# Graph layer with two adjacency relations: from neighbour sums first to weight products first, with a list scheduler

## The chip, the core and the metric

The kernel runs on one core of one Trainium2 chip. The metric is the device time of a whole execution in microseconds, the median of several runs. A shape such as 128x256 in a profile row is partitions x elements per partition.

## The reference, cut to what matters

There are B = 64 graphs of L = 256 tokens with H = 768 features, and a 0/1 adjacency matrix per graph (about 1.6% ones).

```python
h = jnp.maximum(_layernorm(x, axis=-1), 0.0)
...
ctx = jnp.matmul(adj, hs @ Wadj.T + badj) / deg_c[..., None]
ctx = ctx + jnp.matmul(radj, hs @ Wrev.T + brev) / rdeg_c[..., None]
ctx = ctx + hs @ Wself.T + bself
agg = jnp.einsum('bij,bijr->bir', adj, E[rels])
rel = agg @ Wr.T + br * deg[..., None]
...
x = x + (ctx + rel)
```

Here hs is h, radj is adj turned over, deg and rdeg are their row sums, and rels is adj itself. Since adj holds 0 and 1, the relation terms shrink to a few rank-one rows: token degree times a row of length 768. A second program path for other adjacency values (`general_path`) is compiled in and skipped by a branch on a flag.

## The kernel before, in words

Per graph, three 256 x 768 left matrices (the two neighbour sums `A h / deg` and `A' h / rdeg`, and h itself) meet three 768 x 768 weights. `PRODUCTS` is a fast 3x3 block scheme: the 2x3 blocks a0..b2 of left rows (tokens 0-127 are a, 128-255 are b; 0, 1, 2 is which left matrix) times the 3x3 blocks of weights (which relation, which third of the output columns) in 15 products in place of 18. Each product is [128 x 768] by [768 x 256], six matmul steps of contraction 128, and each is added to or taken from several output blocks.

The work is an order written out by hand, in two sweeps over the 64 graphs, because not all combined weights `W[n]` fit beside the rest.

- Sweep 1 (`step1`, `ORDER1`, eight products): while the products of graph M run on PE, `others_of_step` makes the left matrices of graph M+1 (`self_features` L391 on POOL, `aggregate` L400: 24 matmuls 128x512 in fp32r on a high and a low part of h, evicted by DVE at L405), and the statistics, transpose (`spread`, L340) and normalisation (L362) of graph M+2. `combine_left` (L417) builds sums of left blocks on POOL. `store_left` writes the left matrices to DRAM on ACT's queue; partial outputs go out on SP's queue.
- Sweep 2 (`step2`, `ORDER2`, seven products): left matrices and partial outputs come back. From graph 2 on, four of the seven products (9, 7, 15, 4) are done in 12-bit words: `split_left` (L431 to L434) cuts the left operand into three fp32r words, `split_right` has cut the weights, and `product_first` (L457), a rescale of the PSUM bank on ACT (L460) and `product` (L469) add three fp32r products. The other products are fp32 matmuls (L469), which PE executes as two instructions each. `add_out` (L482, L484) adds banks to the output on DVE.
- Rank-one rows are one fp32r matmul each (L474). DMA issues come from SP and ACT.

`spread` also sends per-token factors through DRAM: `d` out (L347), then `row` back, broadcast to all partitions (L349).

Of the kernel before, what the change touches and what calls it, by code (L numbers as in the profile page):

```python
# [9 lines left out]
F32 = mybir.dt.float32  # L10
F32R = mybir.dt.float32r
BF16 = mybir.dt.bfloat16
# [5 lines left out]
P = 128  # L18
EPS = 1e-5
NMEAN, RSTD, RDEG, RRDEG = 8, 9, 10, 11  # L20


STEP = 4096.0
LOWER = 1.0 - 2.0**-13

# [7 lines left out]
    11: ("a1", "-12 +22 +10"),  # L35
# [7 lines left out]
    13: ("a0", "-00 +20 +02"),  # L43
    1: ("b0", "-00 +10 +01"),
# [3 lines left out]
LEFT1 = {  # L48
    "b0+b1": ("b0", ALU.add, "b1", "t0"),
    "b2-a1": ("b2", ALU.subtract, "a1", "t1"),  # L50
    "a1+b1": ("a1", ALU.add, "b1", "t2"),
    "a1+b0+b1": ("a1+b1", ALU.add, "b0", "b0"),
    "a0+a1+b0+b1": ("a0", ALU.add, "a1+b0+b1", "b1"),
    "a2+b2": ("a2", ALU.add, "b2", "a2"),
}
LEFT2 = {
    "a0+a2": ("a0", ALU.add, "a2", "a0"),
    "a1+a2": ("a1", ALU.add, "a2", "a1"),
    "a0+a2+b2": ("a0+a2", ALU.add, "b2", "a2"),
    "b1+b2": ("b1", ALU.add, "b2", "b1"),  # L60
    "a0+a2+b0+b2": ("b0", ALU.add, "a0+a2+b2", "a0+a2"),
}

ROWS = ((0, 1, None), (1, 2, None), (0, None, 2), (0, 2, 0), (1, None, 1), (1, 1, 0))

ORDER1 = (
    (5, "y", None, ((1, 1, 0),)),
    (10, "z", None, ((1, 1, 2),)),  # L70
    (8, "y", None, ((1, 1, 2),)),
    (11, "w", None, ((-1, 0, 2),)),
    (14, "y", 2, ((-1, 0, 2),)),
    (3, "w", 1, ((1, 1, 2),)),
    (13, "y", 3, ((-1, 0, 0),)),
    (2, "z", 0, ((1, 0, 1),)),
)
ORDER2 = (
    (7, "v", None, None),
    (9, "x", None, ((1, 0, 0),)),  # L80
    (15, "u", None, None),
    (7, "v", None, ((1, 0, 1, 2),)),
    (6, "x", None, ((1, 0, 1),)),
    (15, "u", None, ((1, 1, 1, 2),)),
    (4, "t", None, None),
    (12, "x", 4, ((-1, 1, 1),)),
    (4, "t", None, ((-1, 0, 1), (1, 1, 1))),
    (9, "x", None, None),
    (1, "x", 5, ((-1, 1, 0),)),
)  # L90


WORDS = {9: (5, 10), 7: (8, 11), 15: (14, 3), 4: (13, 2)}
LEFT_WORDS = (("x", "t0"), ("a", "a", "t1"), ("adj", "row", "t2"))
# [3 lines left out]
def kernel(  # L98
# [14 lines left out]

# [7 lines left out]
    NB = H // 3  # L146
# [3 lines left out]
    xt_v = x_t.rearrange("b (f p) i -> b p f i", p=P)  # L150
# [10 lines left out]
    others = const.tile([P, B], F32, name="others")  # L161
    flag = const.tile([1, 1], I32, name="flag")

    def main_path(main: ExitStack):
        pool1 = main.enter_context(tc.tile_pool(name="pool1", bufs=1))
        pool2 = main.enter_context(tc.tile_pool(name="pool2", bufs=2))
        pool3 = main.enter_context(tc.tile_pool(name="pool3", bufs=3))
        dram = main.enter_context(tc.tile_pool(name="dram", bufs=3, space=bass.MemoryType.DRAM))
        kept = main.enter_context(tc.tile_pool(name="kept", bufs=1, space=bass.MemoryType.DRAM))
        ps3 = main.enter_context(tc.tile_pool(name="ps3", bufs=3, space=bass.MemoryType.PSUM))  # L170
        ps1 = main.enter_context(tc.tile_pool(name="ps1", bufs=1, space=bass.MemoryType.PSUM))
        sweep = ExitStack()
        ps_sums = sweep.enter_context(tc.tile_pool(name="ps_sums", bufs=2, space=bass.MemoryType.PSUM))

        W = {n: pool1.tile([P, F, NB], F32, name=f"w{n}") for n in PRODUCTS}
        rows = pool1.tile([P, len(ROWS), NB], F32R, name="rows")

        hilo = pool1.tile([P, 2, C, H], F32R, tag="hilo", name="hilo")
        xT = pool1.tile([P, F, L], F32, tag="xT", name="xT")
        tok = [pool1.tile([P, C, NROW], F32, name=f"tok{i}") for i in range(2)]  # L180
        cols = [pool1.tile([P, C, 64], F32, name=f"cols{i}") for i in range(2)]

        def load_weights(products):
            for n in products:
                right = PRODUCTS[n][1]
                k, o = int(right[1]), int(right[2])
                v = (wadj_t, wrev_t, wself_t)[k].rearrange("(f p) o -> p f o", p=P)
                nc.sync.dma_start(W[n], v[:, :, ts(o, NB)])

        single = {right[1:]: n for n, (_, right) in PRODUCTS.items() if len(right) == 3}  # L190
        turned = set()

        def turn(n):

            if PRODUCTS[n][1][0] == "-" and n not in turned:
                nc.scalar.activation(W[n], W[n], AF.Copy, scale=-1.0)
                turned.add(n)

        def combine_weights(n, eng):

            first, *others = PRODUCTS[n][1].split()
            if not others:
                turn(n)
            for k, other in enumerate(others):
                m = single[other[1:]]
                turn(m)
                if other[0] == PRODUCTS[m][1][0]:
                    if first[0] == "-" and k == 0:
                        eng.tensor_tensor(W[n], W[m], W[n], op=ALU.subtract)
                    else:  # L210
                        eng.tensor_tensor(W[n], W[n], W[m], op=ALU.add)
                else:
                    assert first[0] == "+" or k > 0
                    eng.tensor_tensor(W[n], W[n], W[m], op=ALU.subtract)  # L214

        R = {}

        def load_rows():
            sizes = {"full": len(ROWS) * NB, "brow": H, "pick": 2 * P, "eT": NREL}
            work = pool2.tile([P, sum(sizes.values())], F32, tag="X", name="rows_work")  # L220
            wr = pool2.tile([P, 2, H], F32, tag="Xs", name="rows_wr")
            at = 0
            for n, size in sizes.items():
                R[n] = work[:, at : at + size]
                at += size
            for k in range(2):
                R[f"wr{k}"] = wr[:, k, :]
            nc.gpsimd.memset(work[:, : at - NREL], 0.0)
            R["full"] = R["full"].rearrange("p (k n) -> p k n", n=NB)
            R["pick"] = R["pick"].rearrange("p (k n) -> p k n", n=P)  # L230
            brow = R["brow"]
            nc.sync.dma_start(R["eT"], e_t)
            nc.sync.dma_start(R["wr0"], wr_t)
            nc.sync.dma_start(R["wr1"], wrr_t)
            for q in range(4):
                nc.sync.dma_start(brow[q * 32 : q * 32 + NROW, :], bias)

        def prepare_rows():


            eT, brow, pick = (R[n] for n in ("eT", "brow", "pick"))
            wr = R["wr0"], R["wr1"]
            for k, at in ((0, 1), (1, NBASE + 1)):
                to = pick[:, k, :].rearrange("p (q r) -> p q r", q=4)[:, :, 3 + k]
                nc.scalar.activation(to, eT[:, at : at + 1].to_broadcast([P, 4]), AF.Copy)
            for n in range(2):
                pr = ps_sums.tile([P, 512], F32, tag="pa", name=f"pr{n}")
                for k in range(2):
                    nc.tensor.matmul(pr[:, :HO], pick[:, k, :], wr[k][:, ts(n, HO)], start=(k == 0), stop=(k == 1))
                nc.vector.tensor_add(brow[:, ts(n, HO)], brow[:, ts(n, HO)], pr[:, :HO])  # L250

        def place_rows():
            brow, full = R["brow"], R["full"]
            hi = W[1].bitcast(F32R)
            for c in range(C):
                at = slice(c * 64, (c + 1) * 64)
                for k, (of, plus, minus) in enumerate(ROWS):
                    if of == c and minus is None:
                        nc.scalar.activation(full[at, k, :], brow[at, ts(plus, NB)], AF.Copy)
                    elif of == c and plus is None:  # L260
                        nc.scalar.activation(full[at, k, :], brow[at, ts(minus, NB)], AF.Copy, scale=-1.0)
                    elif of == c:
                        nc.gpsimd.tensor_tensor(
                            full[at, k, :], brow[at, ts(plus, NB)], brow[at, ts(minus, NB)], op=ALU.subtract
                        )
            nc.scalar.activation(hi, full, AF.Copy)
            nc.gpsimd.tensor_tensor(rows, full, hi.bitcast(F32), op=ALU.subtract)
            for q in (0, 2):
                at = slice(q * 32, (q + 1) * 32)
                nc.scalar.activation(rows[at], hi[at].bitcast(F32), AF.Copy)  # L270

        S = [{} for _ in range(B)]

        def load_x(b):
            s = S[b]
            s["x"] = pool1.tile([P, C, H], F32, tag="x", name=f"x_{b}")
            nc.sync.dma_start(s["x"], x_v[b])
# [560 lines left out]
```

## Time and profile before

| | us |
|---|---|
| runs (three) | 2934.51, 2949.36, 2957.05 |
| median | 2949.36 |
| profiled execution, span | 2930.6 |
| sweep 1, most graphs, transpose to transpose (L340) | 26.9 |
| sweep 1, the slower graphs | up to 28.5 |
| sweep 2, from the fourth graph on, start of product 7 to the next | 16.6 |
| the first three intervals of sweep 2 | 24.8, 29.3, 25.0 |

The profiled execution is its own run; its span is 2930.6 us, 18.8 us below the median. Rows of groups read: line, engine, operation, output <- inputs, shape, count, then busy us and mean ns of one, then idle time of the engine before them and what ended it. Rows of the timeline read: start us, length us, engine, line, operation. Matmuls are pipelined: the time that one takes from the stream is the distance between starts and not the length shown.

### The profile page before, as it was taken

What the parts mean: (1) busy time and instruction counts of PE and PEld (TensorE: products, weight loads), DVE (VectorE), ACT (ScalarE), POOL (GpSimd) and SP (SyncE); (2) the same over time, 40 slices, a digit from 0 to 9 for tenths busy, and PEclk for the clock granted to TensorE, in tenths of its full rate; (3) what the DMA queues carried; (4) which work ended last, traced back from release to release, by engine and by line L of the source; (5) the groups of instructions that cost most, each with busy time, mean ns of one, the idle gap of its engine ahead of it and who ended that gap; (6) DMA issues with size and microseconds to landing.
All of it is one profiled execution on the core that took longest, in us unless ns stands there. A gap on an engine that the chain in (4) does not pass through costs nothing.

```text
span 2930.6 us, 39745 instructions
## 1 busy us (share of the span) xinstructions
PE 2821.0 (96%) x15002; PEld 2504.8 (85%) x15002; DVE 1748.8 (60%) x2968; ACT 1027.8 (35%) x2045; POOL 1809.4 (62%) x905
## 2 busy tenths in 40 slices
PE   4699999999999999999999999799999999999999
PEld 3588888888888888888888888689999999999998
DVE  6655555555555655556556663666666666666665
ACT  3222223223223223322223221244445444444443
POOL 4566677676666676766666666355555555555553
PEclk8899999999999999999999999999999999999999
DMA  8667777677677677776666665466766666676664
GB/s 286 226 221 243 249 250 252 238 246 251 234 249 244 229 245 254 248 238 239 227 244 232 233 237 200 172 232 239 250 236 247 243 238 249 234 252 236 245 242 155
DMA packets 226444, 695.08 MB, mean 237 GB/s; under 512 B 17332, under 2 KB 94900, under 8 KB 209864
## 3 DMA queue, kind: packets, MB, share of 16 engines
q1 hardware_dynamic: 189384, 390.49, 40.2%
q10 hardware_dynamic: 36864, 302.01, 27.0%
q8 instruction: 120, 1.97, 0.3%
q14 instruction: 76, 0.62, 0.1%
HBM read 436.31 MB, written 256.11 MB: 236 GB/s over the span
## 4 chain that ended last, share of the span: by engine, by line
PE 78%; POOL 6%; DMA 6%; DVE 5%; ACT 3%; issue 1%; ACTq 0%; SPq 0%; POOLq 0%; DVEq 0%
PE x L469 18%; PE y L469 18%; PE w L469 9%; PE pa L400 8%; PE z L469 7%; POOL xT L391 6%; DMA row<-d 4%; PE x L457 3%; PE u L457 3%; PE v L457 3%; PE t L457 3%; PE t L469 2%; PE u L469 1%; PE v L469 1%; ACT a L309 1%; DVE cols L330 1%
## 5 line engine op out<-in xcount | busy, mean ns | idle before, releaser
L417 POOL TENSOR_TENSOR X<-X,Xs 128x768 f32<-128x768 f32 x256 | 469.6, 1853 | 500.0 <-DVE words L433 435.6
L391 POOL TENSOR_TENSOR xT<-xT,row 128x1536 f32<-128x1536 f32 (+1 forms) x128 | 445.9, 3484 | 192.0 <-DMA row<-d 187.0
L469 PE MATMUL y<-w,X 128*128 128x256 f32 x2304 | 534.7, 382 | 4.6 <-POOL X L417 4.1
L469 PEld LDWEIGHTS y<-w,X 128*128 128x128 f32 x2304 | 431.3, 191 | 71.2 <-POOL X L417 4.9
L400 PE MATMUL pa<-a,hilo 128*128 128x512 f32 x1536 | 453.3, 431 | 27.2 <-DVE X L405 24.1
L392 ACT ACTIVATE Xs<-xT 128x1536 f32<-128x1536 f32 x64 | 95.0, 1485 | 856.3 <-POOL xT L391 817.4
L469 PE MATMUL x<-w,X 128*128 128x256 f32 x1560 | 362.1, 382 | 14.7 <-POOL X L417 10.0
L400 PEld LDWEIGHTS pa<-a,hilo 128*128 128x128 f32 x1536 | 291.9, 191 | 91.1 <-DVE X L405 26.3
L469 PEld LDWEIGHTS x<-w,X 128*128 128x128 f32 x1560 | 289.6, 192 | 50.6 <-POOL X L417 10.4
L405 DVE TENSOR_TENSOR X<-pa,row 128x512 f32<-128x512 f32 x384 | 264.3, 689 | 112.8 <-PE pa L400 111.5
L432 ACT ACTIVATE top<-words 128x768 f32<-128x768 f32 x248 | 202.3, 816 | 248.9 <-DVE words L434 245.4
L362 DVE SCALAR_TENSOR_TENSOR hilo<-x,cols,hilo 128x768 fp32r<-128x768 f32 x128 | 261.8, 2046 | 9.6 <-ACT hilo L365 9.5
L434 DVE SCALAR_TENSOR_TENSOR words<-words,top 128x768 fp32r<-128x768 f32 x248 | 236.5, 954 | 8.6
L433 DVE TENSOR_TENSOR words<-X,top 128x768 fp32r<-128x768 f32 x186 | 177.1, 952 | 43.3 <-POOL X L417 34.9
L322 POOL TENSOR_TENSOR cols<-cols,half 128x2 f32<-128x2 f32 x64 | 44.8, 700 | 246.4 <-DVE cols L321 226.9
L469 PE MATMUL y<-w,b0+b 128*128 128x256 f32 x768 | 176.4, 379 | 2.6 <-POOL b0+b L417 2.6
L469 PE MATMUL z<-w,Xs 128*128 128x256 f32 x768 | 178.0, 382 | 0.0
L469 PE MATMUL z<-w,b2-a 128*128 128x256 f32 x768 | 176.2, 379 | 1.4 <-DVE w L214 1.4
L469 PE MATMUL w<-w,X 128*128 128x256 f32 x768 | 176.3, 379 | 0.0
L469 PE MATMUL w<-w,a1+b 128*128 128x256 f32 x768 | 176.2, 379 | 0.0
L469 PE MATMUL x<-w,Xs 128*128 128x256 f32 x768 | 176.1, 379 | 0.0
L469 PEld LDWEIGHTS z<-w,b2-a 128*128 128x128 f32 x768 | 145.4, 189 | 24.2 <-DVE w L214 1.8
(118 smaller groups left out, 4828.8 us busy)
## 6 DMA issues: line engine op xcount, KB each, us to landing
kept_X<-X ACTq DMA_DIRECT2D x64, 1536.0 KB, 5.1
X<-kept_X ACTq DMA_DIRECT2D x64, 1536.0 KB, 7.2
x<-in_x_dram SPq DMA_DIRECT2D x64, 768.0 KB, 5.2
xT<-in_x_t_dram SPq DMA_DIRECT2D x64, 768.0 KB
o<-in_x_dram SPq DMA_DIRECT2D x64, 768.0 KB
kept_Xs<-Xs ACTq DMA_DIRECT2D x64, 768.0 KB, 6.6
sums<-o SPq DMA_DIRECT2D x128, 384.0 KB, 7.0
Xs<-kept_Xs ACTq DMA_DIRECT2D x64, 768.0 KB, 9.4
```

Source lines behind the costliest of these rows:

```text
L322: nc.gpsimd.tensor_tensor(v[:, :, RSTD], v[:, :, RSTD], half, op=ALU.pow)
L362: nc.vector.scalar_tensor_tensor(lo, hx, rstd, hi.bitcast(F32), op0=ALU.mult, op1=ALU.subtract)
L391: eng.tensor_tensor(v, v, row[:, k : k + 1, :].to_broadcast([P, f1 - f0, L]), op=op)
L392: nc.scalar.activation(s["Xs"], xT, AF.Relu)
L400: nc.tensor.matmul(pa, hilo[:, part, c, ts(f, P)], s["a"][:, c, :, :].rearrange("p s i -> p (s i)"), start=(k == 0), stop=(k == 2 * C - 1),)
L405: nc.vector.tensor_mul(s["X"][:, f, :, :].rearrange("p s i -> p (s i)"), pa, s["row"][:, 2:4, :].rearrange("p s i -> p (s i)"))
L417: (eng or nc.gpsimd).tensor_tensor(L[name], L[x], L[y], op=op)
L432: nc.scalar.activation(top, words[0].bitcast(F32), AF.Copy)
L433: nc.vector.tensor_tensor(words[1], value, top, op=ALU.subtract)
L434: nc.vector.scalar_tensor_tensor(words[2], words[1].bitcast(F32), -STEP, top, op0=ALU.mult, op1=ALU.add)
L457: nc.tensor.matmul(ps, l[k][:, f, :], r[2 * k][:, f, :], start=(k == 0 and f == 0), stop=(k == 1 and f == F - 1))
L469: nc.tensor.matmul(ps, l[:, f, :], r[:, f, :], start=(start and f == 0), stop=(row is None and f == F - 1), skip_group_check=not start,)
```

## The change

The kernel is rewritten, with the same 15-product scheme and two sweeps of eight and seven products.

1. Weights come ahead of neighbour sums. The left operand of all 15 products is h itself (`a0..b2` are now thirds of h's features), the three relations stand side by side in the output columns, and each product is [128 x 256] by [256 x 768]. The neighbour sums are taken of the 768-wide results: `aggregate` multiplies adjacency blocks by a high and a low part (`high_low`) of the two neighbour relations' results, in sweep 2, and DVE scales by the inverse degree while adding.
2. All 15 products are in words. Each is three word pairs x two contraction steps x two halves of 384 columns = 12 fp32r matmuls, with a rescale of the bank on ACT between the pairs of different scale.
3. Between sweeps, h and five partial blocks per graph go to DRAM and return.
4. Every operation is recorded with a cost, a rank (due time plus a table `OFFSETS` of shifts by name) and its buffers. `Plan.schedule` orders the operations by list scheduling and assigns buffers; DVE operations with two SBUF inputs and POOL operations are recorded with a lock so that the plan never runs two of them at once. The program is emitted in that order; at run time each engine follows its own order and waits on semaphores.
5. All DMAs are issued by SP. `x_t` is laid out in tiles, and `dynamic_dma_scratch_size=1024` gives most of the DMA scratch to buffers.

The core of the diff:

```diff
-        def aggregate(b, f):
...
-                    nc.tensor.matmul(
-                        pa, hilo[:, part, c, ts(f, P)], s["a"][:, c, :, :].rearrange("p s i -> p (s i)"),
...
+SLOTS = {"W": 24, "B": 17, "T": 6, "A": 3, "S": 6, "Q": 4}
+PERIOD = (17.2, 21.4)
+PREPARE = (6.0, 4.5)
...
+    def split(b, n, s, rank):
+        src = combine(b, s, PRODUCTS[n][0], rank - LEAD - 1.0)
...
+            lambda: nc.scalar.activation(t(w)[:, 0], src[1](), AF.Copy, scale=LOWER),
...
+            lambda: nc.vector.tensor_tensor(t(w)[:, 1], src[1](), t(w)[:, 0].bitcast(F32), op=ALU.subtract), True,
...
+            lambda: nc.vector.scalar_tensor_tensor(
+                t(w)[:, 2], t(w)[:, 1].bitcast(F32), -STEP, t(w)[:, 0].bitcast(F32), op0=ALU.mult, op1=ALU.add
+            ), True,
...
+    def passes(b, n, w, q, pairs, start, stop):
+        r = words[n]
+        for i, (lw, rw) in enumerate(pairs):
+            for f in range(2):
+                for half in range(2):
+                    nc.tensor.matmul(
+                        t(q)[:, half, : H // 2], t(w)[:, lw, f, :], t(r[rw])[:, f, ts(half, H // 2)],
...
+        pe(took(first) + more(first), rank, f"first {n} {b}", reads_of(first), [q], lambda: run(first, place == 0, True, add(first)))
+        act(
+            on_act(H), rank + 1.0, f"scale {n} {b}", [q], [q],
+            lambda: nc.scalar.activation(view(), view(), AF.Copy, scale=scale),
+        )
+        pe(took(second) + more(second), rank + 2.0, f"second {n} {b}", reads_of(second), [q], lambda: run(second, False, True, add(second)))
...
+    def aggregate(b, s, k, pairs, rank):
+        for ic in range(C):
...
+                for c in range(C):
+                    for part in range(2):
+                        for half in range(2):
+                            nc.tensor.matmul(
+                                t(q)[:, half, : H // 2], t(s["a"])[:, c, k, ts(ic, P)], t(pairs[c])[:, part, ts(half, H // 2)],
...
-    nc = _bacc.Bacc("TRN2", target_bir_lowering=False, num_devices=1)
+    nc = _bacc.Bacc("TRN2", target_bir_lowering=False, num_devices=1, dynamic_dma_scratch_size=1024)
```

Per product, the reads of the bank (`read`) add it into blocks of 128x768: four of them in sweep 1 are first writes on ACT, the other four of sweep 1 and ten of sweep 2 are on DVE. `front1` centres h on POOL and normalises it on DVE (128x768 each, two per graph), with the token factors through `d` and `row` as before. `prepare` cuts each combined weight into three words at the start of each sweep (52 DVE operations of 128x768 in sweep 1, 38 in sweep 2).

## The prediction

> **What bounds the kernel now.** I read the page's busy shares first, then the table of stretches for one steady piece of each sweep, then the timeline of PE for what one matmul takes from the stream, then the groups by shape and the timelines of DVE, POOL and SP for prices.
>
> ```profile
> PE 2821.0 (96%) x15002; PEld 2504.8 (85%) x15002; DVE 1748.8 (60%) x2968; ACT 1027.8 (35%) x2045; POOL 1809.4 (62%) x905
> ```
>
> ```profile
> 150.00:688.00 538.00, 538.00 (x2501) 465.40 (x2500) 293.08 (x600) 157.40 (x369) 380.45 (x180) 1.00 0.70 243
> 2100.00:2432.00 332.00, 332.00 (x2210) 313.31 (x2209) 220.45 (x321) 159.56 (x262) 180.65 (x100) 1.00 0.68 242
> ```
>
> The columns are length, busy us of PE, PEld, DVE, ACT, POOL, granted clock, DMA share, GB/s. PE is busy for every microsecond of both stretches (20 graphs each: 26.9 us and 16.6 us per graph) at full clock; no other engine is over 71%. PE is the bound, if its matmuls are also packed:
>
> ```profile
> 109.67 2.22 PE L400 MATMUL pa<-a,hilo 128*128 128x512 f32 x8
> 111.73 2.75 PE L469 MATMUL y<-w,X 128*128 128x256 f32 x12
> 114.13 0.47 PE L474 MATMUL y<-rows,tokT 128*128 128x256 f32 x1
> 114.44 1.09 PE L400 MATMUL pa<-a,hilo 128*128 128x512 f32 x4
> 115.37 1.46 PE L469 MATMUL w<-w,a1+b 128*128 128x256 f32 x6
> ```
>
> ```profile
> 2001.09 1.59 PE L457 MATMUL u<-w,words 128*128 128x256 f32 x12
> 2002.52 0.87 PE L469 MATMUL v<-w,words 128*128 128x256 f32 x6
> ```
>
> Starts give the price. Fp32r, 512 wide: (115.37 - 114.44)/4 = 0.233. Fp32r, 256 wide: (2002.52 - 2001.09)/12 = 0.119. One fp32 product (12 instructions) with its row matmul: 114.44 - 111.73 = 2.71, so 2.59 for the product. Check: sweep 1 is 8 x 2.59 + 3 x 0.12 + 24 x 0.233 = 26.7 (26.9 seen), sweep 2 is 72 x 0.119 + 3 x 2.59 + 2 x 0.12 = 16.6 (16.6 seen). So 64 x 43.5 = 2784 of 2930.6 us is packed PE work. The other 147 us are the start (some 65), slower graphs in sweep 1 (up to 28.5 instead of 26.9; together 31), the first three intervals of sweep 2 (79.1 - 49.8 = 29), and rests at the end.
>
> **The change, part by part.**
>
> *PE work.* All fp32 products go. Per graph sweep 1 has 8 x 12 = 96 fp32r matmuls of 384 columns, sweep 2 has 7 x 12 + 32 (neighbour sums) + 6 (rows) = 122. No row has an fp32r matmul of 384; between 0.119 at 256 and 0.233 at 512 the straight line gives 0.176, and I take 0.177. Sweep 1: 96 x 0.177 + 0.2 for a transpose = 17.2. Sweep 2: 122 x 0.177 + 0.2 = 21.8. Together 39.0 against 43.5: -4.5 us per graph, 64 x 4.5 = -288 us. Here the Trainium skill (TensorE: Matmul & The Clock Gate, Back-to-back issue gap) says that a warm matmul takes N/2.4 + 2.5 ns: 162 ns at 384, 35.5 us per graph, and 220 us less in all than my 64 x 39.0 = 2496. Its rule fits the fp32 rows here (two passes of 256 in 0.216), but both fp32r rows stand 9% above it; the change is all fp32r, so I use the rows.
>
> *DVE, ACT, POOL.* The prices:
>
> ```profile
> L417 POOL TENSOR_TENSOR b0+b<-X 128x768 f32<-128x768 f32 x64 | 115.9, 1811 | 77.3 <-DVE X L405 77.3
> L432 ACT ACTIVATE top<-words 128x768 f32<-128x768 f32 x248 | 202.3, 816 | 248.9 <-DVE words L434 245.4 <-DVE o L484 1.4
> L433 DVE TENSOR_TENSOR words<-X,top 128x768 fp32r<-128x768 f32 x186 | 177.1, 952 | 43.3 <-POOL X L417 34.9 <-ACT top L432 8.3
> L482 DVE TENSOR_TENSOR o<-o,x 128x256 f32<-128x256 f32 x128 | 53.9, 421 | 162.3 <-PE x L469 162.2
> ```
>
> Busy us, then mean ns. DVE, sweep 1: 16 word cuts of 256 x 0.42 = 6.7; 4 reads of 768 x 0.95 = 3.8; 2 normalisations x 0.95 = 1.9; statistics 4 x 0.54 (L319) + 0.6 = 2.7: 15.1 of PE's 17.2. Sweep 2: 14 x 0.42 + 10 reads x 0.95 + 4 sums x 0.95 + 4 small x 0.2 = 20.0 of 21.8. In the trace independent DVE operations start 0.08 before the one ahead ends (L482 at 1002.44 + 0.42, the next at 1002.77), which takes off up to 2.4 and 2.6. DVE rises from 60% to 78-90%: under PE, with little to spare. ACT, sweep 1: 8 rescales and 4 first writes x 0.82, 8 first words x 0.37 (L460), 0.3: 13.1. Sweep 2: 11 x 0.82 + 7 x 0.37 + 6 conversions x 0.59 (L309 with its accumulator read) + 0.6 = 15.7. Under PE. POOL: 1.81 at 768 and 3.50 at 1536 (L391) give 0.70 at 256. Sweep 1: 6 x 0.70 + 2 x 1.81 + 0.70 (L322) = 8.5; sweep 2: 5 x 0.70 + 4 x 1.81 = 10.7.
>
> *DVE against POOL.* Today words are cut with one operand in PSUM (L433: 952 with POOL running or not). The new cuts and normalisations have two SBUF inputs, like L362, alone 1.01 (three cases at the start), mean 2.05:
>
> ```profile
> 1002.77 2.22 DVE L362 SCALAR_TENSOR_TENSOR hilo<-x,cols,hilo 128x768 fp32r<-128x768 f32 x1
> ```
>
> ```profile
> 1002.36 1.82 POOL L417 TENSOR_TENSOR a1+b<-X 128x768 f32<-128x768 f32 x1 [0.57 <-PE w L469]
> 1004.26 2.41 POOL L417 TENSOR_TENSOR X<-a1+b,X 128x768 f32<-128x768 f32 x1
> ```
>
> DVE is issued at 1002.77 and ends at 1004.99, 0.81 after POOL's end at 1004.18; POOL's next takes 2.41 instead of 1.82, 0.59 longer, though DVE still had 0.73 to run. The Trainium skill (SBUF — State Buffer, Who interferes with whom) says that the pair is held for the whole instruction. By that rule sweep 1 needs 16 x 0.42 + 1.9 + 8.5 = 17.1 us of the pair per graph, as much as PE's 17.2, and the plan would have to be perfect. By the row DVE gives it back about 0.15 early: 16 x 0.27 + 2 x 0.80 + 8.5 = 14.4. Sweep 2: 16.6 by the rule, 14.5 by the row, of 21.8. I take the row, with some stalls left (below).
>
> *Turn-around of a bank.* In sweep 2 today ACT starts 0.32 after the start of a product's last word matmul, which is 0.20 after its 0.119 slot, and PE can go on 0.05 after ACT. With a rescale of 0.82 that is 1.07 us between the two parts of a product. In the emitted order, the work that PE does before it returns to the same bank is 8 matmuls (1.42 us) at three returns of sweep 1 and 12 (2.12) or more at the others; sweep 2 is alike. So it fits when ACT is free, with 0.35 to spare at the shortest.
>
> *DMA.* Per graph sweep 1 moves 11 pieces of 0.39 MB and 0.26 for the row: 4.6 MB; sweep 2 4.5 MB. The stretches show 243 GB/s at a share of 0.70, 347 GB/s if full: 13.2 us of 17.2, and 12.9 of 21.8. All issues now stand in one queue, 13 per graph and sweep at about 0.37 us, 4.8 us. Each `row` holds it until `d` has landed:
>
> ```profile
> 862.16 0.93 SPq L347 DMA_DIRECT2D d<-line  x2
> 866.33 0.35 SPq L349 DMA_DIRECT2D row<-d  x1
> ```
>
> 3.9 us after the second `d` at 862.48. Behind it wait loads of x and h and stores of partial blocks, and for these DVE's statistics and POOL. The order puts two transfers (2.3 us of work) between `d` and `row`, so about 1.6 us of the engines' time is lost: 14.8 of 17.2. Hidden; if the cover goes it costs what exceeds 17.2. Smaller scratch: every issue in the new order is on SP, none on POOL, so I count it as nothing.
>
> *Start, middle, end.* `prepare` in sweep 1 is 52 DVE operations of 768. Back to back a 1536-wide one takes 1.67 (30.78 to 32.45, L214), so 0.87 each: 45 us, plus 6 for the first graph's own cuts and 11 for the statistics of five graphs that stand between them. DVE starts near 10, waits for DMA at first, and ends near 75 us. Only one graph and part of the second are done then: 55 lost, about as now (65). Sweep 2: 38 x 0.87 = 33, of which some goes under the last graphs of sweep 1: 28 lost, as now (29). End: last sums, adding, store and its landing (5.1 in the DMA issues): 10. Together 93.
>
> **The sum.** 64 x 39.0 = 2496, + 93 = 2589. Stalls: between none and 5 us per graph (rival B in full). Today's far less tight sweep 1 loses 31/64 = 0.5; I take 0.7, 45 us in all: 2634 as a profiled span. The profile's span is 18.8 us (0.6%) under the median of the runs, so the median would be 2650.
>
> **Rivals.**
>
> A, the forecast: PE stays the bound at 39.0-40.5 us per graph. For it: packed PE today, all other sums under PE's. 2590 to 2720.
>
> B, DVE and POOL hold each other up. For it: the row of L362, which doubles in nearly every case, and 32 such operations per graph. Against: the plan knows the lock, and the waits in today's trace repeat in the same places for every graph. If in each graph the 6 long POOL operations cost DVE half their time, 0.9, and the 11 short ones 0.35, DVE gets 9.3 us: 35.1 + 9.3 = 44.4 without overlaps, 39.4 with them. The middle, 41.9, is 2.9 over PE: 2589 + 64 x 2.9 = 2775, range 2720 to 2860.
>
> C, the one SP queue is late in sweep 1. For it: 14.8 of 17.2 and all stores in order. Against: nothing in sweep 1 loads what was just stored, except `row`. At 3.5 us over PE's 17.2: 2589 + 64 x 3.5 = 2813; 2720 to 2850.
>
> D, slower: the bank turn-around. If ACT has two other 0.82 operations ahead of a rescale, the 1.07 grow to 2.71, and three returns at 1.42 and five at 2.12 stall PE by 3 x 1.3 + 5 x 0.6 = 6.9 us in sweep 1, about 5.5 in sweep 2: 12.4 per graph, 2589 + 794 = 3383. It turns the sign from (2949 - 2589)/64 = 5.6 us per graph on, 0.37 us at each of 15 products. Against: ACT is at 72-76%, and its queue rarely holds two long ones in a row.
>
> E, the new words win nothing because fp32r matmuls with their loads don't hold 0.177 at 384 (0.20 would be enough): 64 x 218 x 0.023 = 321, 2910 + stalls, no change.
>
> **Chances.** A 0.62, B 0.21, C 0.08, E 0.03, D 0.06. The time is A's, 2650. A's own range 2590 to 2720; the range for 8 in 10 leaves out D, E and the upper part of B, and takes in a lower stall and a shorter start: 2570 to 2810. About 1% is what a measurement of this kernel can tell from no change. Faster by over 1% are A, B, C: 0.91; within 1% E: 0.03; slower D: 0.06.
>
> **What would show it.** PE starts 0.177 apart within a group of four; steady graphs 17.2-18 us apart in sweep 1 and 21.8-22.5 in sweep 2; PE busy all through them; DVE 78-90%. B would show as word cuts (256 wide) well over 0.42 and PE's longest waits on DVE; C as waits for `x`, `xt` or `row` landings; D as waits of PE on ACT's rescale. The forecast falls if a steady graph takes over 41 us, or if the start or middle lose over 40 us more than said.

## The result, and the profile after

| | us |
|---|---|
| before, median on the same chip | 2949.42 |
| after, median of four runs (2752.92 to 2768.15) | 2760.02 |
| ratio, with 95% interval | 0.9372 (0.9335 to 0.9409) |
| profiled execution of after, span | 2756.2 |
| sweep 1, mean distance from graph to graph (transposes L492, sixth to last but one) | 18.80 |
| sweep 2, the same (transposes L625) | 22.37 |

The change saves 6.3%. The forecast was 2650 with 2570 to 2810 around it; the time lies in the range, but 110 us above the point, and above the 2720 at which the likeliest case ended. It is rival B's size.

The top of the page of after, with the shares of the engines:

```profile
span 2756.2 us, 43346 instructions
PE 2545.2 (92%) x14090; PEld 2439.7 (89%) x14090; DVE 2444.6 (89%) x4013; ACT 1698.2 (62%) x3459; POOL 1322.4 (48%) x1160
```

Two stretches of after, one inside each sweep (length, busy us of PE, PEld, DVE, ACT, POOL, granted clock, DMA share, GB/s):

```profile
150.00:1100.00 950.00, 884.06 (x4910) 849.43 (x4909) 877.54 (x1466) 604.23 (x1063) 468.26 (x453) 0.99 0.72 245
1300.00:2600.00 1300.00, 1267.44 (x7077) 1219.60 (x7078) 1126.78 (x1851) 794.30 (x1827) 646.43 (x519) 1.00 0.58 197
```

Before, PE was busy in every microsecond of such stretches. Now it rests for 7% of the first and 2.5% of the second. DVE is busy for 92% of the first, a share that includes the time in which an issued operation only waits. The timeline of PE in sweep 1 of after gives the price of one matmul:

```profile
706.36 1.55 PE L406 MATMUL w<-word,left 128*128 128x384 f32 x8
707.75 1.55 PE L406 MATMUL y<-word,left 128*128 128x384 f32 x8
709.13 0.86 PE L406 MATMUL z<-word,left 128*128 128x384 f32 x4
```

The starts are 1.39 and 1.38 apart for eight matmuls: 0.173 each, where 0.177 was forecast. So PE is not slower than said; it waits. The waits of PE, over the whole execution of after (us in total, times, longest):

```profile
PE y L406 <- DVE c L462: 55.4, 35, 2.7
PE pt L492 <- POOL cols L489: 39.0, 3, 30.7
PE pt L625 <- DVE c L460: 26.1, 43, 1.7
PE y L406 <- DVE left L395: 16.4, 2, 15.9
PE w L406 <- DVE x L462: 12.8, 23, 1.6
```

Apart from the two lines with the waits of 30.7 and 15.9 us (the start), PE waits for DVE to read a product out of its PSUM bank (L460, L462), since the next product goes into that bank. Those reads are not slow themselves, as the groups of after by shape show (busy us, mean ns of one, idle before):

```profile
L395 DVE SCALAR_TENSOR_TENSOR left<-left 128x256 fp32r<-128x256 f32 x960 | 524.0, 552 | 25.9
L391 DVE TENSOR_TENSOR left<-b2-a,left 128x256 fp32r<-128x256 f32 x64 | 57.0, 891 | 2.5 <-ACT left L387 2.3
L391 DVE TENSOR_TENSOR left<-a0+a,left 128x256 fp32r<-128x256 f32 x64 | 26.7, 417 | 0.0
L462 DVE SCALAR_TENSOR_TENSOR c<-x,c 128x768 f32<-128x768 f32 x128 | 121.7, 951 | 5.6 <-PE x L406 2.9 <-ACT junk L614 0.5
```

A read takes its 0.95. The word cuts ahead of it in DVE's queue (two per left operand, L391 and L395) don't all take their 0.42: some groups do (417), others take twice that (891). The difference is whether POOL was at work on two SBUF inputs. One place shows it, in the timelines of DVE and then of POOL:

```profile
710.87 1.09 DVE L391 TENSOR_TENSOR left<-b2-a,left 128x256 fp32r<-128x256 f32 x1
712.00 0.85 DVE L395 SCALAR_TENSOR_TENSOR left<-left 128x256 fp32r<-128x256 f32 x1
712.76 2.59 DVE L515 SCALAR_TENSOR_TENSOR h<-h,row 128x768 f32<-128x768 f32 x1
715.28 0.41 DVE L391 TENSOR_TENSOR left<-h,left 128x256 fp32r<-128x256 f32 x1
715.73 0.42 DVE L395 SCALAR_TENSOR_TENSOR left<-left 128x256 fp32r<-128x256 f32 x1
716.07 0.95 DVE L462 SCALAR_TENSOR_TENSOR x<-z,x 128x768 f32<-128x768 f32 x1
```

```profile
709.83 1.85 POOL L511 TENSOR_TENSOR h<-h,row 128x768 f32<-128x768 f32 x1 [1.89 <-PE y L406]
711.64 0.92 POOL L377 TENSOR_TENSOR a0+a1+b0+b<-h,a1+b0+b 128x256 f32<-128x256 f32 x1
712.52 2.02 POOL L511 TENSOR_TENSOR h<-h,row 128x768 f32<-128x768 f32 x1
```

The normalisation (0.95 alone) is issued at 712.76, while POOL's centring runs until 714.54, and ends at 715.35: 2.59. The read of `z` behind it comes 1.6 us late, and PE stops:

```profile
717.08 1.68 PE L406 MATMUL w<-word,left 128*128 128x384 f32 x8 [1.14 <-DVE x L462]
```

Such waits carry no releaser, that is, the profile names nothing that ended them: they are hidden in the length of the instruction, and DVE looks busy. Taking from each DVE operation with two SBUF inputs (L391, L395, L515) what it takes alone (416, 425, 950 ns), DVE lost 197 us of the 1100 between 100 and 1200: 3.4 us per graph. Of these 115 stand beside centrings (L511), 82 beside block sums (L377). In sweep 2, without centrings, it is 57 us of 1400: 0.9 per graph.

In all, a graph takes 18.80 + 22.37 = 41.17 us instead of 39.0, 2.17 over PE's work: 139 us over 64 graphs, where 45 were forecast (+94). What lies around the graphs is 2756.2 - 64 x 41.17 = 121 us, where 93 were forecast (+28). That is the whole miss of the span, 2634 to 2756.

### The profile page after: what moved, and what is told of

Its sections match the earlier page's. It is cut to its first block, busy times and chain, and to the rows that moved or that the text cites. A ratio compares the mean times of both kernels' runs of the same rounds, so it can differ in the third digit from the quotient of the medians.

```text
span 2756.2 us, 43346 instructions
## 1 busy us (share of the span) xinstructions
PE 2545.2 (92%) x14090; PEld 2439.7 (89%) x14090; DVE 2444.6 (89%) x4013; ACT 1698.2 (62%) x3459; POOL 1322.4 (48%) x1160
## 4 chain that ended last, share of the span: by engine, by line
PE 55%; DVE 20%; DMA 12%; issue 7%; ACT 5%; SPq 1%; ACTq 0%; POOL 0%; DVEq 0%; POOLq 0%
PE x L406 14%; PE agg L656 11%; PE y L406 7%; DVE left L391 6%; PE t L406 5%; PE z L406 4%; DMA kept<-c 4%; PE w L406 4%; PE v L406 3%; PE u L406 3%; DVE c L460 2%; DMA c<-kept 2%; ACT c L451 2%; DVE stats L481 2%; DVE h L515 2%
## 5 line engine op out<-in xcount | busy, mean ns | idle before, releaser
L644 POOL TENSOR_TENSOR hl<-c,hl 128x768 fp32r<-128x768 f32 x256 | 471.7, 1852 | 720.1 <-ACT hl L640 709.8
L406 PE MATMUL y<-word,left 128*128 128x384 f32 x3072 | 616.5, 342 | 80.5 <-DVE c L462 55.4
L406 PEld LDWEIGHTS y<-word,left 128*128 128x128 f32 x3072 | 541.9, 191 | 108.0 <-DVE c L462 67.6
L406 PE MATMUL x<-word,left 128*128 128x384 f32 x3072 | 611.1, 340 | 8.8 <-DVE c L462 3.7
L406 PEld LDWEIGHTS x<-word,left 128*128 128x128 f32 x3072 | 533.8, 189 | 27.7 <-DVE c L462 18.9
L395 DVE SCALAR_TENSOR_TENSOR left<-left 128x256 fp32r<-128x256 f32 x960 | 524.0, 552 | 25.9
L656 PE MATMUL agg<-hl,a 128*128 128x384 f32 x2048 | 398.9, 335 | 1.0 <-DVE c L667 1.0
L656 PEld LDWEIGHTS agg<-hl,a 128*128 128x128 f32 x2048 | 361.0, 188 | 2.6 <-DVE c L667 1.3
L406 PE MATMUL w<-word,left 128*128 128x384 f32 x1536 | 317.0, 341 | 33.2 <-DVE x L462 12.8
L406 PE MATMUL z<-word,left 128*128 128x384 f32 x1536 | 308.6, 342 | 4.9 <-ACT c L451 3.4
L511 POOL TENSOR_TENSOR h<-h,row 128x768 f32<-128x768 f32 x128 | 250.7, 1959 | 90.9 <-DMA h<-in_x_t_dram 23.9
L377 POOL TENSOR_TENSOR a2+b<-h,h 128x256 f32<-128x256 f32 x64 | 50.3, 785 | 469.4 <-DVE h L515 410.9
L391 DVE TENSOR_TENSOR left<-h,left 128x256 fp32r<-128x256 f32 x256 | 138.0, 539 | 39.7 <-ACT left L387 39.3
```

Of the source, the lines that this page charges most:

```text
L391: lambda: nc.vector.tensor_tensor(t(w)[:, 1], src[1](), t(w)[:, 0].bitcast(F32), op=ALU.subtract), True,
L395: lambda: nc.vector.scalar_tensor_tensor(t(w)[:, 2], t(w)[:, 1].bitcast(F32), -STEP, t(w)[:, 0].bitcast(F32), op0=ALU.mult, op1=ALU.add), ...
L406: nc.tensor.matmul(t(q)[:, half, : H // 2], t(w)[:, lw, f, :], t(r[rw])[:, f, ts(half, H // 2)], start=start and i == 0 and f == 0, stop=s ...
L511: lambda h=h, one=one: nc.gpsimd.tensor_tensor(t(h), t(h), one(0), op=ALU.subtract),
L644: lambda: nc.gpsimd.tensor_tensor(t(pair)[:, 1], t(o), t(pair)[:, 0].bitcast(F32), op=ALU.subtract),
L656: nc.tensor.matmul(t(q)[:, half, : H // 2], t(s["a"])[:, c, k, ts(ic, P)], t(pairs[c])[:, part, ts(half, H // 2)], start=(c == 0 and part ...
```

## The experiments

The theory after the result (theory 1): in sweep 1 DVE's cuts wait for POOL's operations with two SBUF inputs, and DVE, so filled, holds PE. Rivals: the reads or ACT's rescales turn the banks around too late (theory 2 in most expectations; in that of the centring it is that POOL itself is late), the single DMA queue, and the plan's costs. Ratios are to before on the same chip; after stands at 0.9372. The runs were spread over several chips, on which before takes 2939 to 2949 us, so differences of some 10 us between medians are read from the ratios.

| run | median us | ratio (95%) |
|---|---|---|
| all POOL work write-only | 2615.6 | 0.8883 (0.8852 to 0.8914) |
| only centring write-only | 2667.48 | 0.9049 (0.9021 to 0.9078) |
| only block sums write-only | 2639.67 | 0.8954 (0.8927 to 0.8981) |
| centring on DVE | 2702.16 | 0.9164 (0.9137 to 0.9191) |
| plan ignores the lock | 2924.23 | 0.993 (0.9905 to 0.9955) |
| plan with the measured costs | 2896.51 | 0.9835 (0.9791 to 0.988) |
| first words in PSUM | 3158.0 | 1.072 (1.0683 to 1.0758) |
| three buffers fewer | 3686.36 | 1.2497 (1.2442 to 1.2553) |
| stores issued by ACT | 2744.95 | 0.9339 (0.9307 to 0.9372) |
| no rescale (single run) | 2733.6 | - |
| last weight word a DVE fill (single run) | 2761.73 | - |
| last weight word a POOL fill | 2747.91 | 0.9313 (0.9279 to 0.9347) |

### POOL's work made write-only: all, centring, block sums

```diff
- lambda: nc.gpsimd.tensor_tensor(t(home), x[1](), y[1](), op=op),
+ lambda: nc.gpsimd.memset(t(home), 1.0),
- lambda h=h, one=one: nc.gpsimd.tensor_tensor(t(h), t(h), one(0), op=ALU.subtract),
+ lambda h=h: nc.gpsimd.memset(t(h), 1.0),
```

The first pair is the block sums, the second the centring; the run with all of it also fills the low parts (L644). A fill writes SBUF and reads nothing. It is also shorter than what it replaces (0.74 us for the centring's 1.96), so POOL gets faster too. But in after no wait of PE, DVE or ACT between 150 and 1100 us is for a POOL operation, so lateness of POOL is not what these runs take away.

> POOL's block sums, its centring of h and its low parts are replaced by memsets of the same tiles, so that POOL writes and reads nothing (layer norm's mean, block sums and low parts are left out); order and all else unchanged. Theory 1, DVE's two-SBUF-input operations wait for POOL and this makes DVE the bound of sweep 1: their waits (197 us in sweep 1, 57 in sweep 2 of the changed kernel's trace) vanish, sweep 1 goes from 18.8 to 17.0-17.4 us per graph, sweep 2 from 22.3 to about 22.0, total 2620-2660 us. Theory 2, PE loses its time at the turn-around of the banks (rescale on ACT, read on DVE), whatever POOL does: 18.5 us or more per graph in sweep 1, total over 2720.

> Of the two kinds of POOL work that read two SBUF inputs in sweep 1, only the centring (128x768) is replaced by a fill that reads nothing; it leaves out the mean in layernorm. Theory 1 (VectorE's cuts wait for POOL's two-input operations): the centrings account for 115 us of VectorE's 197 us of waits between 100 and 1200 us, some 126 us over 64 graphs; the run without any such POOL operation won 144 of about 270, so between half and nearly all of the 126 comes back: 2645 to 2700 us, and VectorE's 256-wide cuts in sweep 1 fall from means of 570 and 660 to about 480 and 540 ns. Theory 2 (POOL itself is late, its operations being long): POOL is busy for half of sweep 1, so shortening two of its operations gives less than 15 us, 2745 to 2760.

> The block sums (128x256, 11 per graph in both sweeps) alone are replaced by fills that read nothing; it leaves out the sums, so the products take constants. Theory 1: they account for 82 us of the waits in sweep 1 and 51 in sweep 2, some 142 us over 64 graphs; with half of it won back, 2660 to 2710. If waits of a quarter of a microsecond each are absorbed by the slack between VectorE and the products, as sweep 2 suggests, then only sweep 1's share of half of 90 shows: 2710 to 2735. The sum of the gains of this run and of the run that leaves out only the centring should be near 144 if the two kinds bind separately, above it if either alone is enough.

The stretch of sweep 1, in the run with all three, in that with the centring and in that with the sums:

```profile
150.00:1100.00 950.00, 938.16 (x5324) 917.55 (x5322) 786.29 (x1592) 657.58 (x1158) 205.71 (x493) 1.00 0.78 267
```

```profile
150.00:1100.00 950.00, 936.17 (x5285) 910.58 (x5284) 824.44 (x1583) 652.37 (x1146) 371.46 (x495) 1.00 0.78 265
```

```profile
150.00:1100.00 950.00, 939.82 (x5287) 908.97 (x5287) 860.83 (x1581) 649.23 (x1146) 342.48 (x490) 1.00 0.77 265
```

Per graph (mean distance; DVE's busy share times the distance; DVE's waits behind POOL):

| | sweep 1 us | DVE busy | of it waits | sweep 2 us |
|---|---|---|---|---|
| after | 18.80 | 17.4 | 3.4 | 22.37 |
| centring write-only | 17.43 | 15.1 | 1.0 | 22.38 |
| sums write-only | 17.51 | 15.9 | 1.5 | 21.81 |
| all write-only | 17.30 | 14.3 | 0.0 | 21.83 |
| centring on DVE | 17.95 | 17.2 | 1.5 | 22.45 |

Without POOL's reads the graphs take 17.30 and 21.83: the 17.2 and 21.8 that the forecast gave PE's work. The waits are what stands between. PE is busy for 98.8% of the stretch in that run. The gain of all three is 144 us, a little more than expected. The centring alone gives 93 us, inside its range. The sums alone give 120, more than either expected range: a miss in size. It splits into 64 x 1.29 = 83 us in sweep 1 and 64 x 0.56 = 36 in sweep 2, so the quarter-microsecond waits of sweep 2 were not absorbed, as had been thought possible, but are nearly the whole of its excess. The two gains add to 213, over 144: in sweep 1 it is enough to take away either kind. With DVE busy for up to 15.9 us a graph is at most 0.2 longer than the 17.30; with 17.2 and 17.4 it is 0.65 and 1.5 longer.

### The centring issued by DVE

```diff
- lambda h=h, one=one: nc.gpsimd.tensor_tensor(t(h), t(h), one(0), op=ALU.subtract),
+ lambda h=h, one=one: nc.vector.tensor_tensor(t(h), t(h), one(0), op=ALU.subtract),
```

> The centring is issued to VectorE (0.95 us) where the plan has it on POOL (1.96 us), in the plan's place; nothing is left out and the order is the same. Theory 1: VectorE gains 2 x 0.95 = 1.9 us of work per graph in sweep 1 and loses 2 x 0.98 = 2.0 us of waits behind POOL, so the time stays: 2735 to 2775. If the wait behind POOL is not what holds sweep 1, VectorE's share of it goes from 92 to about 102 per cent and sweep 1 grows by over 1.5 us per graph: 2850 to 2880. If the length of the centring on POOL is what delays the next graph, the shorter one gives 2690 to 2720.

It computes all that the reference does and is the fastest such version measured: 2702.16, 58 us less than after. Theory 1's own number (2735 to 2775, no change) missed. Its arithmetic was right for DVE, as the stretch and the waits of PE in this run show:

```profile
150.00:1100.00 950.00, 923.26 (x5153) 885.12 (x5152) 911.50 (x1646) 635.94 (x1117) 286.26 (x371) 1.00 0.75 258
```

```profile
PE pt L492 <- POOL cols L489: 38.3, 3, 29.5
PE pt L625 <- DVE c L460: 30.9, 49, 1.7
PE y L406 <- DVE c L462: 18.9, 47, 2.3
```

DVE's time per graph hardly changes, 17.2 for 17.4. But PE's largest wait for DVE's reads (`y`, L462) falls from 55.4 us to 18.9. What changed is the size of the pieces. Between 150 and 1100 us after has 60 DVE operations that waited over 0.8 us each (1.2 per graph), this run none. Take as a gap of PE the distance between two starts less the slot of 0.173, where more than 0.2 is left. In after, 64 of the 80 us of gaps end within 4 us after such an operation, while these 4 us cover only 25% of the time. Those 64 us are 1.3 per graph; in this run all gaps come to 42 us, and a graph is 0.85 shorter. With the sums write-only, 57 such waits remain, yet PE's gaps fall to 14 us in all: a long wait is absorbed where DVE has 1.6 us of slack per graph. So these runs point to both together: DVE near its limit, and a wait of 1 to 2 us ahead of a read that PE needs. The rival whose number was hit, that the length of the centring delays the next graph, has no wait in either trace to stand on: neither PE's nor DVE's waits name the centring in the steady part. Since the edit shortens the centring and moves it at once, the two are not separated by a run of their own.

### The plan: lock left out, costs corrected

```diff
- wait = o.known > now + 1e-9 or (o.lock and locked > now + 1e-9)
+ wait = o.known > now + 1e-9
```

> The plan ignores the lock between DVE and POOL (one condition of the list scheduler taken out), so the order of instructions changes; the work is the same. Theory 1: waits of DVE for POOL grow from 254 us in the steady stretches to 350 or more, total 2800-2900 us. If the lock in the plan is of no use, because at run time POOL runs ahead of the plan anyway: 2735-2780. Theory 2 says nothing but small changes, 2735-2780.

```diff
- return 0.15 + 0.00105 * n
+ return 0.07 + n / 960.0
- return 0.16 + 0.00086 * n
+ return 0.11 + 0.00079 * n
- return 0.1 + 0.0023 * n
+ return 0.19 + 0.00213 * n
- return 0.006 + 0.000447 * n
+ return 0.0024 + 0.000445 * n
```

(DVE, ACT, POOL, PE; and 0.12 more for L395.)

> The plan's costs are set to the distances between starts that the trace shows (DVE 0.07 + n/960, ACT 0.11 + 0.79n/1000, POOL 0.19 + 2.13n/1000, PE 0.173 at 384, and 0.12 more for the third word, which waits for the second); work and lock rule are the same, the order changes, the table of shifts stays. If DVE waits for POOL because the run drifts from the plan: waits under 150 us, total 2660-2730. If the table of shifts fits only the old costs: 2760-2900.

Without the lock in the plan, the kernel is 164 us slower than after, more than expected (20.0 and 23.7 us per graph). The loss as a whole can't be booked as the worth of modelling the lock. In sweep 1 DVE's waits behind POOL are 2.9 us per graph there, less than after's 3.4, though a graph takes 1.2 longer. In sweep 2 they rise from 0.9 to 2.5, three quarters of it beside the low parts (L644), and a graph takes 1.3 longer: that part fits the lock. Costs nearer to the trace, with the lock kept, also lose 137 us, with waits of 2.4 and 2.2 us per graph. One reading is that the table of offsets fits one set of costs, so that each change of the plan spoils its fit; no run fitted the table anew. The runs show that a changed order costs some 140 to 160 us, not by which part of it.

### First words kept in PSUM, so that a cut has one SBUF input

```diff
+ act(
+     on_act(2 * P), rank - LEAD + 0.2, f"top {n} {b}", [(w, 0)], [top],
+     lambda: nc.scalar.activation(t(top), t(w)[:, 0].bitcast(F32), AF.Copy),
+ )
- lambda: nc.vector.tensor_tensor(t(w)[:, 1], src[1](), t(w)[:, 0].bitcast(F32), op=ALU.subtract), True,
+ lambda: nc.vector.tensor_tensor(t(w)[:, 1], src[1](), t(top), op=ALU.subtract),
```

`top` lies in columns of the same four bank pairs that the products leave free; the second cut is changed alike.

> Each cut of a left operand gets one more ACT copy that puts the first word into the unused 128 columns of two PSUM banks; both DVE operations of the cut then have one SBUF and one PSUM operand. The result is the same as before. ACT gets 15 x 0.37 = 5.5 us more per graph. Theory 1: DVE's cuts take 0.42 with POOL or without, sweep 1 goes to 17.0-17.5 us per graph, total 2630-2680 us. Theory 2: ACT has more in front of its rescales, so PE waits longer: over 2756.

A miss for theory 1's number, and a loss of 398 us against after. The cuts (L396 and L400 in that kernel) take at most 0.425 us everywhere, so with one operand in PSUM they no longer wait for POOL. But the copies (L392) now wait for PE's work in the same bank, the first cuts (L396) for the copies, and PE's matmuls (L411) for the second cuts (L400). PE also waits for the rescales (L447), as the other expectation said it would behind the added copies. From the list of all waits of this run, and from that of PE:

```profile
DVE left L396 <- ACT bank L392: 299.9, 258, 4.0
ACT bank L392 <- PE bank L411: 182.5, 201, 3.2
```

```profile
PE bank L411 <- DVE left L400: 125.2, 128, 14.9
PE bank L411 <- ACT bank L447: 94.7, 73, 2.1
```

The new waits take the place of the old ones and are larger. The products take all four bank pairs of the kernel, so a pair of its own for the words would have to be taken from them; that wasn't run.

### Three word buffers fewer

```diff
- SLOTS = {"W": 24, "B": 17, "T": 6, "A": 3, "S": 6, "Q": 4}
+ SLOTS = {"W": 24, "B": 14, "T": 6, "A": 3, "S": 6, "Q": 4}
```

> The 3 KB buffers go from 17 to 14, three of the five that the smaller DMA scratch makes room for; the plan orders anew. If this part of the change is worth nothing, as predicted: 2730-2785 us. If the plan needs them to run ahead of PE: over 2800, with waits of DVE and ACT for DMA landings or for freed buffers.

926 us slower than after, far outside what was expected. In the list of waits POOL's centring now waits for its load (23.9 us in after):

```profile
POOL h L511 <- DMA h<-in_x_t_dram: 565.1, 76, 31.2
```

Part of the loss may be the order, which was fitted to 17 buffers, and the granted clock is lower too (0.89 to 0.90 in sweep 1, 0.99 in after); the run doesn't separate these. The old size of the DMA scratch as a whole, with as many buffers fewer as that takes, wasn't run: with 12, five fewer, the planner finds no order. But counting the smaller scratch as nothing was wrong as an account of the change: its room is what the plan is built on.

### Stores by ACT, and no rescale

```diff
- lambda h=h, k=k: nc.sync.dma_start(t(k), t(h)))
+ lambda h=h, k=k: nc.scalar.dma_start(t(k), t(h)))
```

The same for the five partial blocks.

> In sweep 1 the seven stores per graph (h and the five partial blocks) are issued by ACT in place of SP; the order is the same. Rival C, the one SP queue is late in sweep 1: sweep 1 falls to about 17.2 us per graph, total 2650-2690. Theory 1, DVE waiting for POOL is what binds sweep 1: no gain, 2745-2800, with a small loss since seven issues take 2.5 us of ACT per graph.

```diff
- lambda: nc.scalar.activation(view(), view(), AF.Copy, scale=scale),
+ lambda: None,
```

This one leaves out the scaling of the small words' sums.

> The rescale of each bank on ACT between the two parts of a product is not emitted (the weighting of the word pairs is left out); ACT loses 15 x 0.80 us per graph and PE no longer waits for it. Theory 2 or rival D, the turn-around binds: PE's waits go, sweep 1 at 17.2 us or less per graph, total under 2670. Theory 1: DVE's waits for POOL stay near 254 us in the steady stretches, total 2715-2770.

The stores: 0.9339 against 0.9372, with intervals that overlap: some 10 us, and a graph of sweep 1 still takes 18.52, not the 17.2 that the queue as the cause would give. Rival C's 160 us are not there. The rescale: some 20 us less in a single run, with 18.69 us per graph in sweep 1 and 0.3 less in sweep 2 (22.07), though ACT loses 12 us of work per graph. So the turn-around of the banks, rival D, is hidden in sweep 1 as forecast, and nearly so in sweep 2; in after PE's largest wait on it is this one:

```profile
PE x L406 <- ACT x L442: 1.4, 1, 1.4
```

### The start: the weights' last word

```diff
- lambda f=f, h=h: nc.vector.scalar_tensor_tensor(
-     t(w[1])[:, f, :], t(w[0])[:, f, :].bitcast(F32), -1.0 / STEP, t(h), op0=ALU.mult, op1=ALU.add
- ), True,
+ lambda f=f, h=h: nc.gpsimd.memset(t(w[1])[:, f, :].bitcast(F32), 0.0), True,
```

Both runs leave out that word of the weights (`word1`, the second of three by number and the last to be made); the first has the fill on DVE (`nc.vector.memset`).

> In preparing the weights, the second words (30 DVE operations of 128x768 with two SBUF inputs) are replaced by memsets (the second words of the weights are left out). If DVE's preparation sets the start and the middle: 16 x 0.6 = 10 us less before the steady part of sweep 1 and up to 8 us less in the middle, total 2735-2747 beside 2756. If the row through DRAM or DMA sets the start: 2750-2760. The steady graphs stay at 18.8 and 22.3.

> The last word of each prepared weight (30 operations of 128x768, 0.95 us each, 16 at the start and 14 in the middle) is a fill on POOL instead of a VectorE operation; it leaves out that word of the weights. VectorE is busy 19.5 of 20 us in each of the stretches 20:40, 40:60 and 60:80, so if its preparation sets the start, the end of the first graph's wait on VectorE at 78.56 us moves to about 64, and the middle shortens by up to 12: 2730 to 2742. If the start is set by the loads of the weights or by the statistics, less than 5 us: 2755 to 2762.

The first decided nothing: DVE's fill took 0.70 and freed too little. The stretch from 60 to 80 us in after, and then in the second run:

```profile
60.00:80.00 20.00, 3.06 (x8) 2.58 (x9) 19.52 (x29) 9.91 (x15) 0.00 (x0) 0.50 0.00 0
```

```profile
60.00:80.00 20.00, 10.16 (x49) 9.78 (x49) 15.34 (x20) 9.72 (x16) 9.21 (x8) 0.70 0.12 49
```

In after DVE is full (19.5 of 20) while POOL and DMA do nothing and PE gets 8 matmuls. The long wait of PE on L395 ends at 78.6 in after and at 69.1 here, and PE's 200th matmul begins at 104.9 instead of 115.0: 10 us, less than the 15 expected. The median falls by 12 us with intervals that still overlap. So DVE's preparation holds PE at the start, but only part of its lateness is shown to come from there.

## Why the prediction was right and wrong

*PE's work: right.* 39.0 us per graph were forecast, and the run without POOL's reads comes to 17.30 + 21.83 = 39.13. The slot is 0.173; the 0.004 saved on each matmul doesn't show in the sum, and where it goes wasn't traced. The Trainium skill's 162 ns, which its page (TensorE: Matmul & The Clock Gate, Back-to-back issue gap) gives for an isolated warm matmul, is too low here, as it was for before's fp32r rows.

*ACT, DMA, SP, bank turn-around: right.* PE's waits on a rescale are at most 1.4 us long, its list of waits names no DMA, and taking the rescales away, or the stores off SP's queue, moves little.

*The stall term: wrong, and this is the step that failed.* "Today's far less tight sweep 1 loses 31/64 = 0.5; I take 0.7". It measured 2.17 per graph, 94 us more. The prediction had the mechanism (rival B), its instructions and its price from L362, and even DVE's share of 78 to 90% (89). It then compared the pair's occupancy with PE's time, 14.4 of 17.2, and took the rest for room. But the lock is a wait inside an in-order queue: a cut that stands behind a 2 us centring delays the read behind it, whatever the mean. The rule that the pair is held for the whole instruction stands on the page that the prediction cites (SBUF — State Buffer, Who interferes with whom) with DVE's two-port modes; of two SBUF inputs the page says that they contend with POOL's reads, and that is what the traces show. B's sum was 2.9 us per graph over PE and landed at 2775; the measured 2.17 is three quarters of it. B's split was off: it had 3.9 us of DVE's waits in sweep 1 and 5.4 in sweep 2, where 3.4 and 0.9 were measured. Its "half their time" for a long operation fits the centrings (0.98 of 1.96) but not the low parts of sweep 2, beside which only 6 us of waits stand in all.

That the plan knows the lock, the reason held against B, was true and not enough. In sweep 2 it keeps the cuts clear of the low parts (6 us of waits, 107 in the run that ignores the lock), but in sweep 1 it leaves 1.2 long waits per graph. Why it leaves them isn't settled: with corrected costs there are 0.9 per graph, and both sweeps are longer. That the time fell inside the stated range owes something to the width of the range; the forecast's own sign of falling, a steady graph of over 41 us, came true with 41.17.

*The start: mis-sized.* The forecast let DVE's preparation end near 75 us (77.4) but held "one graph and part of the second" done by then; PE had begun 39 matmuls, less than half a graph. PE's 200th matmul, about two graphs of work or 35 us, begins at 115.0: 80 lost, not 55. That is most of the 28 us around the graphs.

*Scratch as nothing: wrong as an account, without effect on the sum*, because the order that was costed already had the buffers.

## What to carry to other kernels

Where an operation of one engine makes one of another engine wait, don't compare summed occupancy with the period; look at the longest single hold, at what is queued behind it on the in-order engine, and at how much slack that engine has. Moving one long two-input operation from POOL to DVE, though DVE was the fullest engine, gained 2% here: what it cost in work it gave back in waits, and the long waits were gone. And a change of the planner also changes an order that was fitted by hand, so its run may measure the fit as well as the change.

## What the runs showed of the hardware

- A 128x256 cut with both inputs in SBUF took 0.42 us alone and up to 2.1 behind POOL's 128x768 operation; with one input in PSUM none of 1920 took over 0.425.
- A POOL fill of SBUF beside such cuts costs them nothing (no waits in the run with all POOL work write-only, and sweep 2's cuts at means of at most 425 ns with the sums write-only).
- A DVE fill of 128x768 fp32 took 0.70 us, three quarters of an operation with two inputs (0.95).
- Fp32r matmuls started 0.173 us apart at 384 columns, between 0.119 at 256 and 0.233 at 512, at a granted clock of 0.99 to 1.00.
